# Score and weighted-sum tiles in pairs, and a table of ranks, in a four-layer graph attention kernel

## The chip, the cores and the metric

The kernel runs on one core of a Trainium2 chip. Its time is the device time of one execution in microseconds (us); lower is better. TensorE (PE) multiplies, VectorE (DVE), ScalarE (ACT) and GpSimd (POOL) do the elementwise work, and SyncE (SP) issues most of the transfers.

## The reference

`x` has 128 graphs of 64 nodes with 512 features each, `adj` says for each graph which nodes see each other. Four layers follow one another, each with a residual:

```
h = relu(layernorm(x));  x = x + layer_l(h, adj)
layers 0 and 2: q, k, v = h@Wq, h@Wk, h@Wv          (4 heads of 64)
                softmax(where(adj, q k^T / 8, -max)) v  @ Wo + bo
layer 1:        a second layernorm (gamma, beta), 8 heads of 64, out projection 512 x 512
layer 3:        m = h@map^T + b;  n = m normalized per head;  cos = n n^T > 0.1, masked
                p = softmax(where(mask, -1e10, (m@q^T)(m@k^T)^T / 8)), masked
                out = relu((cos * p) (h@gcn^T + b) @ W^T / (sum(cos * p) + 1))     (8 heads of 64)
```

All is f32.

## The kernel before

**Tiling.** The 8192 rows of `x` make 16 groups `s` of 512 rows: 8 graphs, two to a block of 128 rows, four blocks to a group. A step is a pair (layer, group). `x` goes back to memory between layers.

**One step.** `loads` fetches `x`; `layernorms` normalizes; `transposes`, `moves` and `turned_tokens` turn the tokens into `hT`. The projections are done by `winograd`: seven products of half-size blocks in place of eight, each of four matmuls (line 636), in the PSUM tiles `mA` (four of the seven, one after another in the same tile, each copied out by ACT before the next begins), `mB` and `mC` (added by DVE, line 666). `front` then takes the mask (`masks`) and makes the scores (`scores`, line 954): matmuls on quarters of the array, 64 x 64, four side by side, 32 of them to fill a `sc` tile of two PSUM banks. Layers 0 and 2 have one such unit for a group, layers 1 and 3 two. `softmax_parts` (965 to 984) masks the tile, takes the maximum and, in layers 1 and 3, subtracts it into `E`, after which the `sc` tile is free; in layers 0 and 2 ACT's exponential reads the tile sixteen times. `divide` (997) scales the rows on POOL. `turns` brings `E` into its transpose `F` (eight ACT copies, line 1006, and a DVE transpose, 1010). `attention` makes the weighted sums `po` (line 1127), again 32 quarter matmuls into a tile of the same ring as the scores, copies them out and multiplies by the output weights. In layer 3 `front` also makes the cosines, which fill a `sc` tile too and are read by `neighbours` (1234), and `last` makes `po3` (1272), which `finish` (1179) adds to the residual. `norms` (896) gives the lengths for the cosines, `add_rows` (869) adds a bias row to the layer 3 values.

**PSUM.** Eight banks: one `sc` tile of two, three `ma` tiles and three `mm` tiles of one bank each (`mm` holds `mB`, `mC` and some small tiles).

**The order.** Every part of the work is a generator that yields what it needs: an event, or an instruction with an engine and an assumed duration. `Order.run` is a planner that runs while the program is written: it takes the generator whose instruction can start first by its own clock and, among equals, the one with the smaller `prio`:

```python
s = min(self.live, key=lambda s: (s.start(self.free), s.prio))
s = self.urgent(s) or s
if eng == "pe":
    at += DRAIN * (self.quads != s.quads())
```

The order in which it takes them is the order of the instructions in each engine's queue, which the chip then keeps. A `Ring` gives tiles out in turn: the n-th tile comes free when its user sets its event. What one generator writes between two yields stays together; `scores` and `attention` yield once for every 8 matmuls and `last` for every 4 (`quads`), so that others can come between.

Of the kernel before, what the change touches and what calls it, by code (L numbers as in the profile page):

```python
# [14 lines left out]
P = 128  # L15
D = 512
N = 64
# [9 lines left out]

DRAIN = 0.1

# [45 lines left out]
class Order:  # L75
# [13 lines left out]
    def step(self, s):  # L89

        self.now = s.ready
        while True:
            try:
                r = next(s.gen)
            except StopIteration:
                self.live.remove(s)
                return
            if isinstance(r, Event):
                if r.t is None:
                    s.op = None  # L100
                    self.live.remove(s)
                    r.waiting.append(s)
                    self.held.add(s)
                    return
                s.wait_for(r.t)
                self.now = s.ready
            else:
                s.op = r
                return
# [101 lines left out]
def gnn_stack(ctx: ExitStack, tc: tile.TileContext, a: dict, out: bass.AP):  # L211
# [32 lines left out]
    ps = bass.MemoryType.PSUM  # L244
    r_sc = ring("sc", 1, [P, 2, 512], space=ps)
    r_ma = ring("ma", 3, [P, 512], space=ps)
    r_mm = ring("mm", 3, [P, 512], space=ps)

# [99 lines left out]
    def weights():  # L348
        for key, parts in units:
            if key == "q1":  # L350
                yield p_ready[0, 0]
# [104 lines left out]
    def loads(steps):  # L456
        for l, s in steps:
            if l > 0:
                yield x_done[l - 1, s]
# [22 lines left out]
    def layernorms(steps, half):  # L482

        for l, s in steps:
            yield l_ready[l, s, half]
            whole, xe = loaded.pop((l, s, half))
# [9 lines left out]
    def turned_tokens(l, s):  # L496
# [25 lines left out]
        moved = od.event()  # L522
        od.spawn(part(blocks[:3], moved), 3)
        yield from part(blocks[3:], None)
# [14 lines left out]
    def moves(steps):  # L539

        fe = None
        for l, s in steps:
            for half in range(2):
                yield n_ready[l, s, half]
# [29 lines left out]
    def transposes(steps):  # L574

        for l, s in steps:
            if (l, s) in by_dma:
                h = yield from by_vector(l, s)
            elif (l, s) in turned:
                h = yield from turned_tokens(l, s)  # L580
            else:
                h, h_done[l, s] = yield from r_h.new("hT")
                hT[l, s] = h
# [158 lines left out]

    def unit(A, BT, tokens_out, out_):

        used, begun = od.event(), od.event()
        od.spawn(winograd(A, BT, tokens_out, out_, used, begun), 5)
        yield begun
        return used

    st, p_ready, s_ready, p_used, o_used, turn = {}, {}, {}, {}, [], []  # L750

    def projections(steps):
        for l, s in steps:
# [4 lines left out]
            if l in (0, 2):  # L758
                yield w_ready[f"qk{l}"] if (l, s) != (0, 0) else first_w
                qk, z["qk_done"] = yield from r_qk.new("qk")  # L760
                used = yield from unit(W[f"qk{l}"], (*BT, w_sums[f"qk{l}"]), False, Out(quarters(qk)))
                od.spawn(when([used], s_ready[l, s], w_done[f"qk{l}"] if end else None), 0)
# [4 lines left out]
                def vv(i, k, V=V):  # L767
                    return V[:, 2 * k:2 * k + 2, i * P:(i + 1) * P]
                es = [used, (yield from unit(v_part(W[f"vo{l}"]), (*BT, wv_sums[l]), True, Out(vv)))]
                z["v"] = V  # L770
                od.spawn(when(es, p_ready[l, s], t_done[l, s], h_done[l, s]), 0)
            elif l == 1:
                es = []
                for n in "qk":
                    yield w_ready[f"{n}1"]
                    o, z[f"{n}_done"] = yield from r_qk.new(f"{n}T")
                    es.append((yield from unit(W[f"{n}1"], (*BT, w_sums[f"{n}1"]), False,
                                               Out(quarters(o)))))
                    od.spawn(when([es[-1]], w_done[f"{n}1"] if end else None), 0)
# [5 lines left out]
                def vv(i, k, V=V):  # L785
                    return V[:, 2 * k:2 * k + 2, i * H:(i + 1) * H]
                es.append((yield from unit(W["v1"], (*BT, w_sums["v1"]), True, Out(vv))))
                z["v"] = V
# [22 lines left out]
    def map_part(s, z):  # L811
        yield w_ready["map3"]
        if s == 1:
# [3 lines left out]
        z["m_ready"] = yield from unit(W["map3"], (*hB[3, s], w_sums["map3"]), False,  # L817
                                       Out(quarters(mT), map_b))
        z["m_sums"], z["n_ready"], z["m_used"] = od.event(), od.event(), od.event()
        od.spawn(when([z["m_ready"]], w_done["map3"] if s == NG - 1 else None), 0)  # L820
        od.spawn(sums_after(z["m_ready"], quarters(mT), z, z["m_sums"], s == NG - 1), 1)
        lengths.append(z["n_ready"])
        od.spawn(norms(mT, s, z["m_ready"], z["n_ready"], z["m_used"]), 3)

    lengths = []

    def of_map(n, s, z, bias):
# [4 lines left out]
        z[f"{n}_ready"] = yield from unit(W[f"{n}3"], (quarters(z["n"]), z["T"], w_sums[f"{n}3"]),  # L832
                                          False, Out(quarters(o), bias))

# [7 lines left out]
    def sem_part(s, z):  # L842
# [4 lines left out]
        def sv(i, k):  # L847
            return V[:, 2 * k:2 * k + 2, i * H:(i + 1) * H]
        used = yield from unit(W["sem3"], (*hB[3, s], w_sums["sem3"]), True, Out(sv))
        rows = od.event()  # L850
# [90 lines left out]

    def scores(lT, rT, npair, blocks):
        S, e = yield from r_sc.new("sc")
        nb = len(blocks)
        for b, t in enumerate(blocks):
            for c in range(npair):
# [3 lines left out]
                for g in range(2):  # L950
                    k = slice(t * P + g * N, t * P + (g + 1) * N)
                    for par in range(2):
                        r = slice(par * N, (par + 1) * N)
                        nc.tensor.matmul(S[g * N:(g + 1) * N, par, col],  # L954
                                         lT[r, c, k], rT[r, c, k], start=True, stop=True)
        return S, e

# [141 lines left out]
    def units_of(l):  # L1099
# [3 lines left out]
        return nch, [list(range(u, u + per)) for u in range(0, TB, per)]  # L1103

    def attention(l, s):
        z = st.pop((l, s))
# [3 lines left out]
        got = {("e", k): od.event() for k in range(2)}  # L1110
        od.spawn(residuals(l, s, w_ready[wkey], got), 2)
        O, oe = yield from r_m.new("oT")
        O = O.rearrange("p c t -> p (c t)")
        for u, blocks in enumerate(units):
            yield z["pt_ready", u]
            pt, pte = z["pt", u]
            po, poe = yield from r_sc.new("po")
            for b, t in enumerate(blocks):
# [13 lines left out]
            if u == len(units) - 1:  # L1132
                z["v_done"].set()

            yield act(1.02)
            nc.scalar.copy(O[:, u * 1024:(u + 1) * 1024].rearrange("p (i g q) -> p g i q", g=2, q=N),
                           po.rearrange("p g (i q) -> p g i q", q=N))
            poe.set()
        O = O[:, 0:1024 * len(units)].rearrange("p (k c n) -> p k c n", k=2, n=H)

# [9 lines left out]
        if o_used:  # L1150
            yield o_used.pop()
        used = yield from unit(wo, (ov, T, w_sums[wkey]), True, Residual(got))
        o_used.append(used)
# [34 lines left out]
    def front(l, s):  # L1188
# [8 lines left out]
        masked = [od.event() for _ in units]  # L1197
        od.spawn(when(masked, me), 0)
        for u, blocks in enumerate(units):
            E, e = yield from r_e.new("E")  # L1200
            S, se = yield from scores(z["q"], z["k"], 2 * nch, blocks)
            if u == len(units) - 1:
# [3 lines left out]
            m = mask[:, blocks[0]:blocks[0] + len(blocks)]  # L1206
            z["e", u], z["exp", u] = (E, e), od.event()
            od.spawn(softmax(l, z, u, S, se, m, masked[u]), 1)
        if l < 3:
            return  # L1210
        yield z["n_ready"]
        found = [od.event() for _ in units]
        od.spawn(when(found, nfe), 0)
        for u, blocks in enumerate(units):
            C, ce = yield from scores(z["n"], z["n"], 4, blocks)
            if u == len(units) - 1:
                z["m_done"].set()
            nfv = nf[:, blocks[0]:blocks[0] + 2, :].rearrange("p b k -> p (b k)")
            od.spawn(neighbours(z, u, C, ce, nfv, found[u]), 1)

# [32 lines left out]
    def last(s):  # L1253
        z = st[3, s]
        got = {("e", u): od.event() for u in range(2)}
        od.spawn(last_residuals(s, got), 2)
        for u in range(2):
            yield z["pt_ready", u]
            pt, pte = z["pt", u]
            yield p_ready[3, s]  # L1260

            po, poe = yield from r_sc.new("po3")
            for b in range(2):
# [17 lines left out]
    def fronts(steps):  # L1281
        for l, s in steps:
            yield from front(l, s)

    def turns(steps):

        for l, s in steps:
            yield p_used[l, s]
            z = st[l, s]
            for u in range(len(units_of(l)[1])):  # L1290
                yield z["e_ready", u]
                z["pt", u] = yield from transposed(*z["e", u])
                z["pt_ready", u].set()

    def attentions(steps):
        for l, s in steps:
            yield p_used[l, s]
            if l < 3:
# [5 lines left out]
    for k in steps:  # L1304
        for e in (p_ready, s_ready, p_used, h_ready, f_ready, x_done):
            e[k] = od.event()
        for half in range(2):
            l_ready[(*k, half)], n_ready[(*k, half)] = od.event(), od.event()
    with tc.manual_schedule():
        od.spawn(weights(), 4)  # L1310
        od.spawn(loads(steps), 4)
        for half in range(2):
            od.spawn(layernorms(steps, half), 4)
        od.spawn(moves(by_dma), 3)
        od.spawn(transposes(steps), 3)
        od.spawn(projections([k for k in steps if k[0] < 3]), 5)
        od.spawn(fronts(steps), 1)
        od.spawn(turns(steps), 1)
        od.spawn(attentions(steps), 2)
        od.run()  # L1320
# [45 lines left out]
```

## Time and profile before

| | |
|---|---|
| median of 3 runs | 2753.67 us (2753.2 to 2754.24) |
| profiled execution | 2752.83 us, span of its instructions 2750.6 us |
| PE busy | 2682.1 us, 98% of the span |
| DVE, ACT, POOL busy | 1950.9, 1885.3, 1608.4 us |
| granted clock, mean over the span | 0.991 |

A busy time is the sum of the stretches in which an engine worked. Idle time of an engine counts only where it makes the one wait that sets the end. A line such as `L636` is a line of the kernel's source; `mA<-hT,w_q` are the tile written and those read; `x8` is how many instructions the row holds. Every f32 matmul of the source is two instructions in the trace. `issue` is time in which nothing was waited for that the trace shows.

### The profile page before, as it was taken

To read this page: it belongs to the slowest core of one execution; us is meant where nothing else is said; L and a number is where in the kernel's file an instruction comes from. 1 tells how busy PE (TensorE), PEld (TensorE's weight loads), DVE (VectorE), ACT (ScalarE), POOL (GpSimd) and SP (SyncE) were. 2 spreads that over 40 slices of the span, in tenths; PEclk is the share of its full clock that TensorE was granted. 3 is DMA by queue.
4 is the path that set the end of the run, shared out by engine and by line. 5 is a ranking of instruction groups with operands and counts; after the bars stand their busy time and mean duration, and the time that the engine had idled before them with its cause. 6 is when DMAs were issued, how large, how long until landed. Compare 5 with 4: busy or idle time off the path is not lost.

```text
span 2750.6 us, 63739 instructions
## 1 busy us (share of the span) xinstructions
PE 2682.1 (98%) x26280; PEld 2323.4 (84%) x26280; DVE 1950.9 (71%) x2836; ACT 1885.3 (69%) x3517; POOL 1608.4 (58%) x1242
## 2 busy tenths in 40 slices
PE   7999999999999999999999999999999999999997
PEld 6888888888888888888898888888888888888876
DVE  6888888676666667665678888747776777667655
ACT  5667677678777777776667676656677666776644
POOL 4776767554445445545666767676565555655533
PEclk9999999999999999999999999999999999999998
DMA  5566663221112112212456665323223322233121
GB/s 164 143 178 142 161 170 106 78 77 65 48 63 78 48 48 71 71 48 96 135 126 167 149 163 150 121 100 88 65 64 87 97 69 64 64 87 87 49 64 47
DMA packets 396978, 267.90 MB, mean 97 GB/s; under 512 B 260496, under 2 KB 305552, under 8 KB 396688
## 3 DMA queue, kind: packets, MB, share of 16 engines
q1 hardware_dynamic: 382176, 249.37, 33.1%
q10 hardware_dynamic: 14512, 14.47, 1.7%
q8 instruction: 206, 3.38, 0.5%
q14 instruction: 84, 0.69, 0.1%
HBM read 166.77 MB, written 67.63 MB: 85 GB/s over the span
## 4 chain that ended last, share of the span: by engine, by line
PE 84%; DVE 7%; ACT 3%; POOL 3%; DMA 2%; issue 1%; SPq 0%; ACTq 0%; DVEq 0%; POOLq 0%
PE mA L636 43%; PE mC L636 21%; PE mB L636 11%; PE sc L954 4%; PE po L1127 2%; PE po L1272 1%; ACT F L1006 1%; ACT E L977 1%; DVE sc L965 1%; DVE mx L971 1%; PE mmn L896 1%; POOL t L346 1%; DVE st L423 1%; POOL E L997 0%; PE ptr L593 0%
## 5 line engine op out<-in xcount | busy, mean ns | idle before, releaser
L1006 ACT COPY F<-E 32x512 f32<-32x512 f32 x768 | 472.5, 615 | 47.5 <-POOL E L997 36.0
L1075 POOL TENSOR_TENSOR xres<-xres,u 128x512 f32<-128x512 f32 x192 | 258.9, 1356 | 246.2 <-ACT u L1070 237.9
L1054 POOL TENSOR_TENSOR xres<-xres,u 128x512 f32<-128x512 f32 x192 | 252.6, 1339 | 40.0 <-DMA xres<-x 27.5
L439 ACT ACTIVATE xin<-xin,rs 128x512 f32<-128x512 f32 x320 | 248.4, 812 | 22.5 <-DVE rs L432 20.3
L519 ACT COPY hT<-xin 32x512 f32<-32x512 f32 x364 | 224.1, 616 | 6.4
L423 DVE BATCH_NORM_STATS2 st<-xin 128x6 f32<-128x512 f32 x320 | 214.1, 669 | 9.5 <-DMA xin<-x 5.2
L430 POOL TENSOR_TENSOR rs<-rs,mhalf 128x2 f32<-128x2 f32 x160 | 115.9, 728 | 132.7 <-DVE rs L428 120.5
L653 ACT COPY v<-mA 128x256 f32<-128x256 f32 (+1 forms) x192 | 94.5, 492 | 137.4 <-PE mA L636 133.7
L346 POOL TENSOR_TENSOR t<-hT,t 128x512 f32<-128x512 f32 x126 | 183.3, 1454 | 8.9
L346 POOL TENSOR_TENSOR t<-hT 128x512 f32<-128x512 f32 x63 | 80.7, 1281 | 168.8 <-DVE hT L529 96.2
L997 POOL TENSOR_TENSOR E<-E,sm 128x1024 f32<-128x1024 f32 x64 | 125.6, 1963 | 85.5 <-ACT xin L439 43.1
L1070 ACT COPY u<-mA 128x512 f32<-128x512 f32 x144 | 84.6, 587 | 116.5 <-PE mA L636 112.0
L1010 DVE STREAM_TRANSPOSE F<-F 128x1024 f32<-128x1024 f32 x96 | 118.4, 1234 | 60.6 <-ACT F L1006 60.6
L991 DVE TENSOR_REDUCE sm<-E 128x16 f32<-128x1024 f32 x128 | 154.9, 1210 | 6.9 <-ACT E L984 5.7
L977 ACT ACTIVATE E<-sc,mx 128x64 f32<-128x64 f32 x512 | 124.9, 362 | 32.7 <-DVE mx L974 32.7
L516 POOL COPY hT<-xin 32x512 f32<-32x512 f32 x84 | 64.4, 766 | 138.1 <-ACT xin L439 135.8
L636 PE MATMUL mA<-w_vo,t 128*128 128x128 f32 (+1 forms) x768 | 135.4, 312 | 8.1 <-ACT v L653 4.2
L636 PE MATMUL mA<-hT,w_qk 128*128 128x256 f32 x512 | 129.3, 392 | 7.5 <-DVE hT L569 6.0
L997 POOL TENSOR_TENSOR E<-E,f 128x1024 f32<-128x1024 f32 x32 | 61.1, 1910 | 111.7 <-DVE f L995 95.0
L636 PE MATMUL mA<-t,w_qk 128*128 128x256 f32 x512 | 122.7, 380 | 1.4 <-DVE t L343 1.4
L869 POOL TENSOR_TENSOR v<-v,gcn_row 128x512 f32<-128x512 f32 x64 | 81.2, 1300 | 71.9 <-ACT v L653 71.9
L636 PEld LDWEIGHTS mA<-w_vo,t 128*128 128x128 f32 x768 | 108.7, 191 | 16.9 <-ACT v L653 5.1
(223 smaller groups left out, 7493.7 us busy)
## 6 DMA issues: line engine op xcount, KB each, us to landing
x<-xres SPq DMA_DIRECT2D x96, 512.0 KB
xin<-x SPq DMA_DIRECT2D x96, 512.0 KB
xres<-x SPq DMA_DIRECT2D x64, 512.0 KB
F<-xin SPq DMA_DIRECT2D x448, 64.0 KB
xres<-in_x SPq DMA_DIRECT2D x32, 512.0 KB
u<-rs SPq DMA_DIRECT2D x128, 128.0 KB
xres<-x SPq DMA_DIRECT2D x64, 256.0 KB
out<-xres SPq DMA_DIRECT2D x64, 256.0 KB
```

Source lines behind the costliest of these rows:

```text
L346: nc.gpsimd.tensor_tensor(o, i0, i1, ALU.subtract)
L423: nc.vector.bn_stats(st, v[:, t, :])
L439: nc.scalar.activation(v[:, t, :], v[:, t, :], func, bias=rs[:, 2, t:t + 1], scale=rs[:, 0, t:t + 1])
L519: nc.scalar.copy(o, v)
L636: nc.tensor.matmul(o, l, r, start=(first and m == 0 and k == 0), stop=(k == KC - 1), skip_group_check=True)
L977: nc.scalar.activation(E[:, i, :], S3[:, i, :], AF.Exp, bias=mx[:, i:i + 1], scale=0.125)
L991: nc.vector.tensor_reduce(o, E, AX.X, ALU.add)
L997: nc.gpsimd.tensor_mul(E, E, sm[:, :, None].to_broadcast([P, 16, N]))
L1006: nc.scalar.copy(F[g * N + 32 * k:g * N + 32 * (k + 1), :, 32 * i:32 * (i + 1)], E[g * N + 32 * i:g * N + 32 * (i + 1), :, 32 * k:32 * (k ...
L1010: nc.vector.transpose(F, F)
L1054: nc.gpsimd.tensor_add(xr[:, t, :], xr[:, t, :], bo[l])
L1075: nc.gpsimd.tensor_add(v, v, both(u))
```

## The change

The PSUM is cut anew: two `sc` tiles (four banks), two `ma` and two `mm`. `front` takes the tiles of both units of a group before it makes the scores of either, so that the planner can put the 64 matmuls in a row; the cosines likewise, and `last` and `attention` the weighted sums. In `attention` the copy out of a `po` tile becomes a generator of its own, `out_of`, so that the second sum need not wait for it. In layers 0 and 2 `front` waits, as the planner sees it, for the transposes of the group before (`pt_done`), so that its scores and that group's weighted sums come at one time. The planner's fixed `prio` numbers give way to a table by kind of work and layer (`RANK`), and its assumed cost of a change between the two kinds of matmul goes from 0.1 to 0.15. No instruction is added or taken away.

```diff
-DRAIN = 0.1
+DRAIN = 0.15
+RANK = {
+    "load": (5.5, 5.5, 3, 5.5),
+    "norm0": (4, 4, 5.5, 4),
+    "norm1": (4, 4, 4, 3.5),
+    "move": (5, 2, 1, 5.5),
+    "turn": (3.5, 3, 1, 3.5),
+    "part": (5, 5, 5, 5),
+    "weight": (0.5, 6, 3.5, 1),
+    "proj": (5, 5, 5, 5),
+    "out": (0.5, 5, 5, 2),
+    "front": (0.5, 0.5, 0.5, 1.5),
+    "soft": (1.5, 4, 1, 1.5),
+    "near": (0.5, 3, 3, 0.5),
+    "trans": (3.5, 2, 5.5, 2),
+    "att": (5, 2, 2, 5),
+    "res": (2.5, 1.5, 5, 6),
+    "msum": (3, 0.5, 1.5, 0.5),
+    "length": (4, 5.5, 2, 1.5),
+}
+def rank(what, l):
+    return Rank(RANK[what][l])
...
+            if isinstance(r, Rank):
+                s.prio = r
+            elif isinstance(r, Event):
...
-    r_sc = ring("sc", 1, [P, 2, 512], space=ps)
-    r_ma = ring("ma", 3, [P, 512], space=ps)
-    r_mm = ring("mm", 3, [P, 512], space=ps)
+    r_sc = ring("sc", 2, [P, 2, 512], space=ps)
+    r_ma = ring("ma", 2, [P, 512], space=ps)
+    r_mm = ring("mm", 2, [P, 512], space=ps)
...
     def loads(steps):
         for l, s in steps:
+            yield rank("load", l)
...
-    def scores(lT, rT, npair, blocks):
-        S, e = yield from r_sc.new("sc")
+    def scores(S, lT, rT, npair, blocks):
...
+    def out_of(O, u, po, poe, copied):
+        yield act(1.02)
+        nc.scalar.copy(O[:, u * 1024:(u + 1) * 1024].rearrange("p (i g q) -> p g i q", g=2, q=N),
+                       po.rearrange("p g (i q) -> p g i q", q=N))
+        poe.set()
+        copied.set()
     def attention(l, s):
...
+        room, copied = [], []
+        for u in range(len(units)):
+            yield z["pt_ready", u]
+        for u in range(len(units)):
+            room.append((yield from r_sc.new("po")))
         for u, blocks in enumerate(units):
-            yield z["pt_ready", u]
             pt, pte = z["pt", u]
-            po, poe = yield from r_sc.new("po")
+            po, poe = room[u]
...
+            copied.append(od.event())
+            od.spawn(out_of(O, u, po, poe, copied[-1]), 0)
+        for e in copied:
+            yield e
...
     def front(l, s):
...
+        room = []
+        if l in (0, 2) and s > 0:
+            yield pt_done[l, s - 1]
+        for u in range(len(units)):
+            z["e", u] = yield from r_e.new("E")
+        for u in range(len(units)):
+            room.append((yield from r_sc.new("sc")))
         for u, blocks in enumerate(units):
-            E, e = yield from r_e.new("E")
-            S, se = yield from scores(z["q"], z["k"], 2 * nch, blocks)
+            S, se = room[u]
+            yield from scores(S, z["q"], z["k"], 2 * nch, blocks)
...
+        room = []
+        for u in range(len(units)):
+            room.append((yield from r_sc.new("cos")))
         for u, blocks in enumerate(units):
-            C, ce = yield from scores(z["n"], z["n"], 4, blocks)
+            C, ce = room[u]
+            yield from scores(C, z["n"], z["n"], 4, blocks)
...
     def last(s):
...
         for u in range(2):
             yield z["pt_ready", u]
+        yield p_ready[3, s]
+        room = []
+        for u in range(2):
+            room.append((yield from r_sc.new("po3")))
...
     def turns(steps):
...
+            pt_done[l, s].set()
...
-        od.spawn(projections([k for k in steps if k[0] < 3]), 5)
-        od.spawn(fronts(steps), 1)
+        od.spawn(projections([k for k in steps if k[0] < 3]))
+        od.spawn(fronts(steps))
```

The streams that took a fixed number when they were started now yield their rank at each step, as `loads` does above.

## The prediction

> **What bounds the kernel now.** I read the page first, then the windows of the stretches that fall behind, then the TensorE timeline of a quiet stretch, and last the chain of waits and the tail.
>
> ```profile
> PE 2682.1 (98%) x26280; PEld 2323.4 (84%) x26280; DVE 1950.9 (71%) x2836; ACT 1885.3 (69%) x3517; POOL 1608.4 (58%) x1242
> PE 84%; DVE 7%; ACT 3%; POOL 3%; DMA 2%; issue 1%; SPq 0%; ACTq 0%; DVEq 0%; POOLq 0%
> ```
>
> TensorE (PE) is busy 98% of the span and is 84% of the chain that ended last; no other engine passes 71%. So time comes off only where PE needs less of it or stands still less. Where it stands still, by stretch:
>
> ```profile
> 60.00:80.00 20.00, 12.91 (x109) 10.29 (x108) 11.99 (x20) 12.87 (x33) 12.84 (x11) 0.83 0.66 152
> ...
> 2600.00:2620.00 20.00, 17.13 (x246) 13.08 (x245) 14.15 (x17) 7.19 (x13) 9.94 (x8) 0.83 0.01 3
> 2660.00:2680.00 20.00, 15.05 (x270) 12.68 (x263) 13.42 (x11) 4.52 (x8) 7.68 (x6) 0.83 0.35 89
> 2720.00:2751.00 31.00, 11.48 (x282) 9.36 (x280) 13.57 (x19) 11.60 (x19) 8.70 (x6) 0.70 0.40 103
> ```
>
> The first number after the stretch's length is PE's busy time; the third from the end is the granted clock. From 600 to 1300 us PE idles 0.5 us in all, so the steady part holds almost no waits. Instead, it pays for changing between whole-array products (128*128) and products on quarters of the array (64*64, `sc` and `po`):
>
> ```profile
> 1001.94 1.89 PE L636 MATMUL mA<-hT,w_q 128*128 128x256 f32 x8
> 1003.76 1.16 PE L1127 MATMUL po<-F,v 64*64 64x64 f32 x64
> 1004.86 1.99 PE L636 MATMUL mB<-hT,w_q 128*128 128x256 f32 x8
> 1006.69 1.89 PE L636 MATMUL mA<-t,w_q 128*128 128x256 f32 x8
> 1008.41 1.89 PE L636 MATMUL mC<-t,w_q 128*128 128x256 f32 x8
> ```
>
> Read the starts. Eight whole-array matmuls follow each other 1.72 us apart (1006.69 to 1008.41). The quarter run starts 1.82 us after its predecessor (0.09 late), the next whole-array group starts 1.10 us after the quarter run, and the one after that 1.83 us later (0.10 late). By the single starts in the trace the 64 quarter matmuls lie 943 ns from first to last, 15.0 ns each, so they need 0.96 us by themselves and 0.14 of the 1.10 is the way back. Going there and back costs 0.09 + 0.14 + 0.10 = **0.33 us per run**; 148 of the 169 runs of 64 that stand cleanly between whole-array products show this within a nanosecond.
>
> Two stops late in the kernel are the score tile itself, which has one buffer:
>
> ```profile
> 2607.88 0.69 DVE m L666
> 2608.58 1.14 DVE mx L971
> 2609.72 0.02 issue
> 2609.74 1.24 DVE E L981
> 2610.97 0.14 issue
> 2611.11 1.20 PE sc L954 x64
> 2612.31 0.02 issue
> 2612.33 1.24 DVE Cf L1234
> 2613.57 0.04 issue
> 2613.61 1.99 PE sc L954 x64
> ```
>
> PE ended its products at 2607.86 and waits for VectorE (DVE) to take the maximum and subtract it (L981), since only then may the next tile overwrite `sc`; then again for L1234. The second run of 64 takes 1.99 instead of 0.96 us: the clock was halved. The same happens at 2660.66 (L965, L971, L981 in a row). Against the pitches above, PE loses 13.0 us between 2600 and 2680, 10.5 between 60 and 80.
>
> **The change, part by part.** The order of instructions on each engine in the changed program can be read without running it. It holds the same instructions, number for number (13,204 matmuls in the source, each f32 one being two in the trace); only their order, the PSUM tiles and the waits differ.
>
> Switches: the order shows 221 quarter runs before and 158 after. By quarters of PE's work: 50 to 57, 51 to 28, 55 to 41, 65 to 32. So "all in one" is true of layer 3 and mostly of layer 1; in much of layer 0 both `sc` and `po` are cut into 8 and 24 matmuls with whole-array products between, which is worse than before. 63 runs x 0.33 = 20.8 us of PE time, and PE has no slack to hide it in.
>
> Up to the end of the last cosine run: two of those runs lie behind it, so 61 x 0.33 = 20.1 less; but 3.0 us of `sem3` products that stood behind it now stand ahead. Net **-17.1**.
>
> From there to the end only one chain counts. Before: cosines end at 2717.0, span ends at 2750.6, 33.6 us. After, from the queues' order and the rows' durations: DVE Cf 1.23, product 1.22, row sum 1.21, two additions to v 1.38, f and reciprocal 0.45, second Cf 1.23, row sum 1.21, four `xres` 2.6 (now ahead of the second product), product 1.22, row sum 1.21, f and reciprocal 0.45: 13.4. Then POOL E 1.9, eight ACT copies 5.0, DVE transpose 1.25, `po3` 2.0, `xres` 1.3, and 5.0 for the stores as now: 16.5. With hand-overs 30.1 us. POOL's row additions for the last v (4.93 us, which delayed E before, 2728.99 to 2733.92) end before E is ready. **-3.5**.
>
> The stops at 2606-2671: two `sc` tiles let the next score start while DVE still works on the last. In the new order the last scores and the cosines of the same group lie 8 to 12 us of PE work apart, and DVE needs about 7.4 for the two subtractions ahead. One place stays tight: scores right behind `po3` (about 1 us short, twice). I take 2 of the 13.0 as remaining: **-11**. Bounds: -13 and 0.
>
> Start and layer 0: PE waited 6 us for `hT` (L569), behind the DMA copies of `xin` to `F`. On SP's queue those copies now come ahead of the second half of the next `xin` and of `xres`; but the ~5 us of `w_k` DMA are still there. And between 100 and 600 PE loses 12.8 us, often 0.4 to 1.8 at the first `vo` products waiting for ACT's copies; by the new order those distances are longer. I take **-5** of 23; bounds -12 and +6 (the same stop a second time).
>
> New stops: at -0, nothing; at most one of the kind above for each of the three layer changes. I take **+4**, the price of the smallest of today's (4.4 us at 1360-1380); bounds 0 and 13.
>
> What is costed at nothing. PSUM: `ma` and `mm` go from three to two tiles. Cover: by the order a new `mC` waits for a DVE addition that lies 6.9 us of PE work back (4.4 for the narrow `vo`), against an ACT copy of 0.6, an addition of 0.69 and at most two DVE instructions of 1.2 ahead; the wait for ACT's copy within a unit (1.7) is the same as before. Uncovered, each of the 224 product units would pay. The Trainium skill speaks against this part: "Perfetto Trace Analysis", section "Matmuls", wants independent groups to rotate through PSUM banks so that evacuation overlaps. All eight banks are still used, four now by scores. By that rule alone, priced with the nearest row (ACT's copy of 0.59, uncovered once per unit), it would cost 224 x 0.6 = 134 us and end near 2850; by the distances it costs none. I take the distances.
>
> `pt_done` puts the scores of s behind the transposes of s-1. It only orders the issue, no semaphore wait is added on `sc`. Scores to `po` of one group shrinks from 37 to 29 us of PE work; DVE, ACT and POOL work between is about 17.5 us by the rows. The waiting scores hold up only the softmax of s. That leaves 11 us of cover; each us short of it would cost 32, one per group of layers 0 and 2. The split evacuation (`out_of`) gives `po` back a run later; its reader, the output product, needs both parts anyway. On POOL every wait of PE lies over 10 us back; nothing there becomes tight.
>
> The clock: in both late stops the granted clock is 0.83 over 20 us, so (1 - 0.83) x 20 = 3.4 us are lost each time. "TensorE: Matmul & The Clock Gate", section "What's actually happening", has full rate return after one busy window of about 3.4 us, a loss of 1.7. With its figure the late stops would be worth 3.4 us less and the result 2724; I keep the trace's.
>
> Sum: -17.1 - 3.5 - 11 - 5 + 4 = -32.6. The profiled execution took 2752.83 us (span 2750.6), 0.84 below the median of the runs; 2752.83 - 32.6 = 2720.2, against the median 2721.
>
> **The rivals.**
> Only the switches and the tail pay: -20.6, and one more stop of 6.8. The waits only move, for a planner that closes one gap opens another. For it: DVE is at 71%, and the scores now come in pairs, 5 us of DVE work each. Against: the gaps between sc and its readers are longer. 2732 to 2740.
>
> Everything goes well: -17.1 - 3.5 - 13 - 12, no new stop: 2708.
>
> Slower: PSUM starvation. PE at the first `mB` or `mC` of a unit, behind DVE's addition, pays from 0.15 us per unit on (32.6 / 224) more than is won; at 0.25 us it is +56 - 32.6 = +23, 2777. For it: waits of PE on DVE rise from 395 to 586. Against: 0.5 us idle in 700 today, and distances of 4.4 to 6.9.
>
> The change doesn't do what it says: in layer 0 it does not, as counted. That is in the sum.
>
> **How the numbers follow.** Likeliest case (2712 to 2730) 0.5; only switches (2730 to 2741) 0.24; all goes well (2704 to 2712) 0.14; stops eat nearly all (2741 to 2759) 0.07; starvation 0.05. Two runs apart by 0.2%, 5.5 us, are what a measurement here can tell from no change. Faster 0.92, same 0.03, slower 0.05. The range 2706 to 2740 leaves out about 0.2.
>
> **What would show it.** In the profile after: PE busy lower by about 20 us; quarter runs of x128 in layers 1 and 3, 2.05 us from their start to the next whole-array product (1.10 for x64 now); granted clock 1.00 from 2570 to 2660; the last `po3` starting some 22 us after the cosines (25 now). PE waits "mC <- DVE" or "mB <- DVE" of many tenths in every unit would prove it wrong; so would granted clock below 0.9 in more than four stretches.

## The result, and the profile after

The changed kernel takes **2716.52 us** (median of 4 runs, 2716.26 to 2716.95) against 2753.95 for the kernel before in the same session: ratio 0.9863, 95% interval 0.9846 to 0.9880. Run a second time in another session it took 2715.74 against 2750.46, ratio 0.9869 (0.9852 to 0.9886). The profiled execution took 2716.46 us, its span is 2714.7 us, 35.9 less than before.

From the page, the busy times and the shares of the chain that ended last:

```profile
PE 2651.8 (98%) x26280; PEld 2316.3 (85%) x26280; DVE 1908.4 (70%) x2836; ACT 1887.6 (70%) x3517; POOL 1612.0 (59%) x1242
PE 92%; DVE 3%; DMA 2%; ACT 1%; POOL 1%; issue 1%; SPq 0%; ACTq 0%; POOLq 0%; DVEq 0%
```

The same 26280 matmuls keep PE busy 30.3 us less, and PE is now 92% of the chain instead of 84%: less of the time is somebody else's. The windows where PE stood still before, and a new one (PE, weight loads, DVE, ACT, POOL, granted clock, DMA share, GB/s):

```profile
60.00:80.00 20.00, 19.81 (x231) 17.79 (x229) 17.22 (x29) 12.35 (x33) 16.98 (x14) 1.00 0.46 126
1290.00:1320.00 30.00, 22.09 (x129) 18.70 (x119) 13.47 (x15) 7.15 (x12) 17.61 (x17) 0.83 0.41 122
2600.00:2620.00 20.00, 20.00 (x97) 16.63 (x96) 9.46 (x14) 16.02 (x31) 10.36 (x3) 1.00 0.19 55
2660.00:2680.00 20.00, 20.00 (x212) 17.53 (x211) 10.31 (x12) 11.14 (x19) 7.71 (x7) 1.00 0.00 1
```

The two late stops are gone (20.00 of 20.00 busy, clock 1.00); the stretch at 60 to 80 has 19.81 us of PE instead of 12.91. A new stop has come at 1290 to 1320: 7.9 us idle. In a quiet stretch TensorE's timeline shows a pair:

```profile
2570.52 2.10 PE L1336 MATMUL po<-v,F 64*64 64x64 f32 x128
2572.54 1.99 PE L673 MATMUL mA<-hT,w_map 128*128 128x256 f32 x8
```

A run of 128 starts at 2570.52 and the next whole-array product at 2572.54: 2.02 us for what took 2 x 1.10 as two runs.

The time can be booked in three terms. PE's losses are what it falls behind the pitches of the prediction (0.216 us per whole-array matmul, 0.015 per quarter, 0.33 per quarter run), summed from its first matmul to its last by the single starts in the trace:

| | before | after | difference |
|---|---|---|---|
| quarter runs, 0.33 us each | 221 | 158 | -20.8 us |
| PE's losses | 69.8 us | 50.5 us | -19.3 |
| first matmul | 11.2 us | 15.2 us | +4.1 |
| span | 2750.6 us | 2714.7 us | -35.9 |

That the terms add up to the span proves nothing: the losses are by their making what the other terms leave. What stands on its own is the number of runs, which can be counted, and the price of one, which section 3 measures.

The losses by stretch: 0 to 600 us went from 30.6 to 21.4, 1300 to 1900 from 11.9 to 21.1, 1900 to 2000 from 5.1 to -0.6 (a little faster than the pitches), 2600 to 2680 from 13.0 to 2.6; each other hundred moved by about 1 us or less.

### The profile page after: what moved, and what is told of

Same layout as the page of the kernel before. It is cut to its first block, busy times and chain, and to the rows that moved or that the text cites. A ratio compares the mean times of both kernels' runs of the same rounds, so it can differ in the third digit from the quotient of the medians.

```text
span 2714.7 us, 63736 instructions
## 1 busy us (share of the span) xinstructions
PE 2651.8 (98%) x26280; PEld 2316.3 (85%) x26280; DVE 1908.4 (70%) x2836; ACT 1887.6 (70%) x3517; POOL 1612.0 (59%) x1242
## 4 chain that ended last, share of the span: by engine, by line
PE 92%; DVE 3%; DMA 2%; ACT 1%; POOL 1%; issue 1%; SPq 0%; ACTq 0%; POOLq 0%; DVEq 0%
PE mA L673 47%; PE mC L673 24%; PE mB L673 12%; PE sc L994 4%; PE po L1177 2%; PE cos L994 1%; PE po L1336 1%; PE mmn L937 1%; DMA xres<-x 1%; PE ptr L630 0%; ACT F L1045 0%; ACT E L1016 0%; DVE sc L1004 0%; POOL xres L1093 0%; DVE mx L1010 0%
## 5 line engine op out<-in xcount | busy, mean ns | idle before, releaser
L1045 ACT COPY F<-E 32x512 f32<-32x512 f32 x768 | 473.4, 616 | 35.7 <-POOL E L1036 24.9
L463 POOL TENSOR_TENSOR rs<-rs,mhalf 128x2 f32<-128x2 f32 x160 | 134.7, 844 | 209.4 <-DVE rs L461 197.2
L378 POOL TENSOR_TENSOR t<-hT 128x512 f32<-128x512 f32 x63 | 82.0, 1301 | 128.8 <-DVE hT L564 46.5
L673 PEld LDWEIGHTS mA<-w_vo,t 128*128 128x128 f32 x768 | 110.5, 191 | 11.4 <-ACT v L690 1.9
L1010 DVE TENSOR_REDUCE mx<-sc 128x16 f32<-128x1024 f32 x96 | 116.9, 1218 | 2.2
```

The lines of the kernel that those rows point to most:

```text
L378: nc.gpsimd.tensor_tensor(o, i0, i1, ALU.subtract)
L463: nc.gpsimd.tensor_tensor(rs[:, 0, :], rs[:, 1, :], mhalf[:, :2], ALU.pow)
L673: nc.tensor.matmul(o, l, r, start=(first and m == 0 and k == 0), stop=(k == KC - 1), skip_group_check=True)
L1045: nc.scalar.copy(F[g * N + 32 * k:g * N + 32 * (k + 1), :, 32 * i:32 * (i + 1)], E[g * N + 32 * i:g * N + 32 * (i + 1), :, 32 * k:32 * (k ...
```

## The experiments

The theory: TensorE pays for each change to quarter products and back; the pairs save those changes, and two score tiles let the late stops go, as long as the planner keeps the waits around the merged runs covered. The rivals: the PSUM cut starves the product units; the second score tile alone, or the table of ranks alone, makes the gain; a change by itself costs nothing, and all the time comes from waits. Five parts of the answer follow.

### 1. Do two `ma` and two `mm` tiles starve PE?

The kernel before, with only this edit; one score tile stays, and two banks are left empty.

```diff
-    r_ma = ring("ma", 3, [P, 512], space=ps)
-    r_mm = ring("mm", 3, [P, 512], space=ps)
+    r_ma = ring("ma", 2, [P, 512], space=ps)
+    r_mm = ring("mm", 2, [P, 512], space=ps)
```

> The kernel before with two mA and two mm tiles in place of three, all else kept (221 quarter runs, as before). Theory (the smaller rings cost nothing): TensorE's waits stay, 2754 within 6 us. Rival (starvation of PSUM): from 0.15 us per product unit on, 224 units, at least +34 us, 2788 or more, with waits of PE at mB and mC on DVE.

Measured: 2754.96 us against 2752.43, ratio 1.0012 (1.0004 to 1.0020). What PE waits for in it (total, times, longest):

```profile
PE po L1272 <- DVE F L1010: 9.7, 1, 9.7
PE mA L636 <- ACT v L653: 7.7, 10, 1.9
```

The large waits are those of the kernel before (10.0 and 7.0 us there). `mC` waits for DVE only twice, 0.8 us in all, and `mB` never, where 224 units that each paid 0.15 us would have given 34 us. The cost is 0.1%, so the starvation is refuted for the kernel before; in the changed kernel no wait of `mB` or `mC` for DVE shows at all.

### 2. One part of the change alone

`b_psum`: the kernel before with the new PSUM cut (two score tiles, two `ma`, two `mm`), tiles still taken one by one, old numbers in the planner.

```diff
-    r_sc = ring("sc", 1, [P, 2, 512], space=ps)
-    r_ma = ring("ma", 3, [P, 512], space=ps)
-    r_mm = ring("mm", 3, [P, 512], space=ps)
+    r_sc = ring("sc", 2, [P, 2, 512], space=ps)
+    r_ma = ring("ma", 2, [P, 512], space=ps)
+    r_mm = ring("mm", 2, [P, 512], space=ps)
```

> The kernel before with the new cut of the PSUM alone (two score tiles, two mA, two mm), the tiles still taken one by one, the old fixed numbers. Its order has 185 quarter runs, so 36 fewer: -11.9 us. Theory (a run costs 0.33 us, stops late in the kernel come from the single score tile): -11.9 and -10 for the stops between 2600 and 2680, but its order puts more of TensorE's waits on ACT close behind the copy that they wait for (sum of the shortfalls 221 us against 72 before, most of it in layers 0 to 1), which costs some of that: 2740 within 12. Rival (the ranks make the gain): 2750 or more.

Measured: 2765.72 us, ratio 1.0066 (1.0041 to 1.0091). The theory's 2740 is missed by 26 us. The rival's number, 2750 or more, holds, but its reason, that the ranks make the gain, does not survive the next run.

`b_rank`: the table of ranks and the assumed 0.15 us in the kernel before, with its one score tile, the tiles taken one by one, and no `pt_done`. The numbers given to the planner change, in this way everywhere:

```diff
-DRAIN = 0.1
+DRAIN = 0.15
+RANK = {...}
...
-        od.spawn(winograd(A, BT, tokens_out, out_, used, begun), 5)
+        od.spawn(winograd(A, BT, tokens_out, out_, used, begun), prio)
```

> The changed kernel's table of ranks and 0.15 on the old cut of the PSUM (one score tile, three mA, three mm), tiles taken one by one, no wait for the transposes of the group before. Its order has 224 quarter runs, three more than before. Theory (the gain is switches and the second score tile): +1.0 for switches, the stops late in the kernel stay, 2752 within 12. Rival (the ranks make the gain): 2725 or less.

Measured: 2798.76 us, ratio 1.0181 (1.0159 to 1.0203): the table alone makes this kernel slower. Both accounts (2752, and 2725 or less) missed it.

`a_flat`: the changed kernel, its pairs and its PSUM cut, with the old fixed numbers written into every column of the table; `pt_done` and the assumed 0.15 us stay.

```diff
-    "load": (5.5, 5.5, 3, 5.5),
-    "norm0": (4, 4, 5.5, 4),
+    "load": (4, 4, 4, 4),
+    "norm0": (4, 4, 4, 4),
...
-    "front": (0.5, 0.5, 0.5, 1.5),
+    "front": (1, 1, 1, 1),
...
-    "att": (5, 2, 2, 5),
+    "att": (2, 2, 2, 2),
```

> The changed kernel with the old fixed numbers in its table, the same in all layers (0.15 kept). Its order has 116 quarter runs, 42 fewer than the changed kernel. Theory (0.33 us per run): switches 105 x 0.33 = 34.7 us below before, but the waits on ACT are nearer than in the changed kernel (132 short ones against 24, shortfalls of 222 us against 27, in layers 0 and 1 above all), so the ranks pay by waits: slower than the changed kernel, 2717 to 2745. Rival (switches are all): 2703, 13.9 us faster than the changed kernel.

Measured: 2743.32 us, ratio 0.9968 (0.9958 to 0.9978), inside the theory's range.

The same booking for all of them, each against the kernel before (the sums come out by their making, as above):

| kernel | quarter runs | runs x 0.33 | losses | first matmul | sum | span measured |
|---|---|---|---|---|---|---|
| `b_psum` | 185 | -11.9 | 94.6 (+24.9) | -0.2 | +12.8 | +13.1 |
| `b_rank` | 224 | +1.0 | 111.6 (+41.8) | +4.2 | +47.0 | +47.0 |
| `a_flat` | 116 | -34.7 | 91.7 (+21.9) | +0.3 | -12.5 | -12.4 |
| changed kernel | 158 | -20.8 | 50.5 (-19.3) | +4.1 | -36.0 | -35.9 |

`a_flat` is the telling row: it has 42 runs fewer than the changed kernel, worth 13.9 us, and its span is 23.5 us longer (its median 26.8). The number of runs is not what decides. What PE waits for most; `b_psum`, then `b_rank`, then `a_flat`:

```profile
PE po L1127 <- DVE F L1010: 22.2, 11, 3.6
```

```profile
PE po L1174 <- ACT E L1016: 20.1, 6, 6.9
```

```profile
PE po L1177 <- DVE F L1049: 20.6, 9, 2.6
```

In all three the weighted sum stands at the head of TensorE's queue too early, but not for the same reason. In `b_psum` and `a_flat` it waits for `F`, the last step of its own softmax. In the kernel before that wait (L1127 for L1010) came once, 0.2 us. Most of it lies in layer 1, and the order there shows why. From the last score matmul of a unit to the first matmul of its weighted sum, both by their starts, median over the 16 groups:

| layer 1 | first unit | second unit | PE idle before a sum of layer 1 |
|---|---|---|---|
| kernel before | 26.3 us | 27.5 us | none |
| `b_psum` | 22.0 | 27.5 and 31.4 in turn | 2.3 to 3.5 us, at seven places from 584 to 1246 |
| `a_flat` | 25.0 and 31.1 in turn | 27.5 and 31.1 in turn | 2.2 to 2.5 us, at seven places from 573 to 1227 |
| changed kernel | 65.2 | 65.3 | 1.4 us, once |

The stops lie at the second unit of every second group, the 27.5 of these rows, and that figure holds the stop: without it only some 25 us of work lie between (27.5 less 2.8 and less 2.2). The kernel before put 27.5 us of work there and did not wait, but it had little to spare: from the end of `F` to the start of the sum it had 0.9 us at the second units (median), the sums that stop have 0.1, and the changed kernel has 16.7.

So with the old numbers the planner, offered a second score tile, puts some sums nearer behind their scores; with the table it lets some 40 us more of other work come between. This is what the table buys, and the second score tile is what makes the distance affordable. In the kernel with one tile (`b_rank`) the sums of layer 0 stand 63 us behind their scores, and their softmax is done 38.7 us ahead of them (medians). They wait all the same, for the tile:

```profile
228.07 0.46 PE L994 MATMUL sc<-qk 64*64 64x64 f32 x16
233.06 3.38 ACT L1016 ACTIVATE E<-sc,mx 128x64 f32<-128x64 f32 x16 [5.10 <-DVE mx L1013]
236.49 1.98 PE L1174 MATMUL po<-F,v 64*64 64x64 f32 x64 [6.89 <-ACT E L1016]
```

The scores of a later group were written into the one tile just ahead of the sum, and the sum gets it only when ACT's sixteen exponentials have read them: 6.9 us idle here, and again at 418. Late scores and cosines wait for the tile too (up to 3.7 us, from 2658 to 2717). In `b_psum` the late stops did go (losses of 3.5 us between 2600 and 2700, where the kernel before has 13.0 between 2600 and 2680), as the second tile was to bring; the early layers cost more. Behind the first matmul, the largest waits of the changed kernel are others:

```profile
PE po L1336 <- DVE F L1049: 12.4, 2, 7.2
PE mC L673 <- ACT u L1109: 7.9, 1, 7.9
```

The first lies in the tail; the second is the new stop. So the parts work together only: cut alone +0.7%, table alone +1.8%, cut and pairs (with `pt_done`) -0.3%, all of it -1.4%.

### 3. What one change of kind costs

The changed kernel, with one whole-array product put between the two score runs (and the two cosine runs) of a pair: 48 places. The product writes into a tile whose 32 quarter products are about to overwrite it.

```diff
+            if u == 1:
+                for _ in range(1):
+                    nc.tensor.matmul(S[:, 0, 0:P], ident, ident, start=True, stop=True)
             S, se = room[u]
```

`d_2` has `range(2)`. The second product changes nothing of the kind, so the difference between the two kernels is the product itself, and what the first adds beyond it is one way there and back.

> The changed kernel with one small whole-array product (128 x 128, two matmuls of 112 ns in the trace) between the two units of a group wherever scores or cosines come in pairs: 48 places in layers 1 and 3, written into the second unit's tile before its scores, which overwrite it. No other instruction moves. It breaks up to 48 paired runs again. Theory (a run costs 0.33 us, by the changed kernel's runs of 128 0.35): 48 x (0.22 + 0.35) = 27 us slower than the changed kernel, about 2744. Rival (the switches are covered and the gain is in the waits): 48 x 0.22 = 11 us or less, 2727.

> As the run with one small product in each of the 48 places, with two of them in a row. It separates the product's own cost from the way there and back. Theory: 10.8 us more than with one, so 2755, and what one costs less this difference, 16 to 17 us, is the price of 48 runs. Rival (the products themselves cost 0.57 each and the switch nothing): 27 us more than with one, 2771.

Measured: `d_1` 2743.46 us, ratio 0.9973 (0.9962 to 0.9984); `d_2` 2754.82 us, ratio 1.0012 (1.0005 to 1.0019). PE's losses stay as they were (50.7 and 51.6 against 50.5), so the added time is all TensorE's own. TensorE's timeline of `d_1`, then of `d_2`:

```profile
2082.72 1.16 PE L994 MATMUL sc<-kT,qT 64*64 64x64 f32 x64
2083.81 0.49 PE L1260 MATMUL sc<-ident 128*128 128x128 f32 x2
2084.22 1.16 PE L994 MATMUL sc<-kT,qT 64*64 64x64 f32 x64
2085.32 1.56 PE L673 MATMUL mB<-hT,w_map 128*128 128x256 f32 x6
```

```profile
2090.22 1.16 PE L994 MATMUL sc<-kT,qT 64*64 64x64 f32 x64
2091.31 0.71 PE L1260 MATMUL sc<-ident 128*128 128x128 f32 x4
2091.95 1.16 PE L994 MATMUL sc<-kT,qT 64*64 64x64 f32 x64
2093.05 1.56 PE L673 MATMUL mB<-hT,w_map 128*128 128x256 f32 x6
```

By the starts in these rows a pair takes 2.60 us with one product and 2.83 with two, and the run of 128 shown above took 2.02. More finely, from the last matmul before the pair to the end of the first eight whole-array matmuls after it, less the pitches of these, a pair takes 2.222 us without a product between (70 of 72 clean pairs of the changed kernel), 2.798 with one (38 of 45) and 3.022 with two. The second product is 0.224, so a way there and back is 2.798 - 2.222 - 0.224 = **0.352 us**. A second way to it, within the changed kernel: a run of 128 takes 2.222, a run of 64 takes 1.288; the 64 further matmuls cost 0.934, and the remaining 1.288 - 0.934 = 0.354 are the change. The prediction's 0.33 was 0.02 short: it measured the pitch of a quarter product from the first to the last start of a run of 64, 15.0 ns, where further ones cost 14.6. 63 runs are 22.3 us instead of 20.8.

### 4. `pt_done`

The changed kernel without the wait of the scores for the transposes of the group before.

```diff
-        if l in (0, 2) and s > 0:
-            yield pt_done[l, s - 1]
```

> The changed kernel without the planner's wait of the scores in layers 0 and 2 for the transposes of the group before. Its order has 133 quarter runs, 25 fewer. Theory (runs and waits trade; by the queues' order the shortfalls of TensorE's waits on ACT grow from 27 to 117 us): 8.9 us less for switches, 15 to 25 more for waits, 2719 to 2735. Rival (the switches decide): 2708.

Measured: 2720.94 us, ratio 0.9888 (0.9872 to 0.9905). Without it the planner makes 133 runs in place of 158, which is worth 25 x 0.35 = 8.8 us, and PE's losses rise from 50.5 to 62.8, most of it in this wait, which the changed kernel has not:

```profile
PE sc L994 <- ACT qk L690: 8.0, 12, 1.0
```

Scores now come as soon as their `q` and `k` are copied, and wait for the copy 12 times. The two profiled spans lie 4 us apart, in opposite terms: the line that was to bring the runs together leaves more runs and fewer waits. The two were not run side by side, and the intervals of their ratios overlap, so that `pt_done` gains time on the whole is not shown; that 25 runs fewer bring no gain is.

### 5. The new stop at 1297, and the late start

The chain of waits of the changed kernel at the stop, in order of time:

```profile
1295.55 4.42 DMA xres<-x
...
1300.10 0.42 POOL xres L1093
...
1301.31 1.27 POOL xres L1114
...
1302.61 0.69 DVE xres L703
1303.30 1.14 DVE E L1020
...
1305.43 0.58 ACT u L1109
```

Read from the end: the product waits for ACT's copy `u`; ACT had an exponential ahead of that copy, which needs DVE's `E` (L1020); DVE had `xres` (L703) ahead of `E` in its queue, which waited for POOL, and POOL for the transfer that brings the residual `x` of the last group of layer 1. That transfer starts at 1295.55. SP's queue tells why:

```profile
1277.98 17.53 SPq L590 DMA_DIRECT2D F<-xin  x12
1295.55 1.02 SPq L1089 DMA_DIRECT2D xres<-x  x1
```

It stood behind twelve small copies that took 17.53 us to issue. `r_res` gives the residual of layer 1 a better rank, so that the planner puts its load earlier; the order on PE and the 158 runs are the same.

```diff
-    "res": (2.5, 1.5, 5, 6),
+    "res": (2.5, 0.5, 5, 6),
```

> The changed kernel with one number of the table changed: residual loads of layer 1 at 0.5 in place of 1.5. TensorE's order is the same, 158 runs; on SP's queue the load of the last group's residual at the end of layer 1 now stands ahead of seven of the copies of xin to F. Theory (the stop of 8 us at 1297.8 is that load, held up behind those copies and then by the weights of layer 2): the stop and its halved clock, 10.8 us, go, 2706. Rival (the weights' transfer holds everything up in any order, or the wait is DVE's or ACT's own): 2716 as now.

Measured: 2709.72 us (2705.66 to 2712.22), ratio 0.9847 (0.9831 to 0.9862). Run again beside the changed kernel on the same chip:

> The changed kernel once more, beside the next one on the same chip, so that the two can be compared without the kernel before between them. Theory: 2716 within 4 us, with the stop of 8 us at the end of layer 1 at the same place.

> The changed kernel with the residual loads of layer 1 at 0.5 once more, beside the changed kernel on the same chip. Theory (the stop at the end of layer 1 is a load kept waiting on SP's queue): 7 to 11 us faster than the changed kernel beside it. Rival (the 7 us of the run before were another chip): within 3 us of it.

Measured: changed kernel 2715.74 us (2713.00 to 2717.66), `r_res_2` **2707.22 us** (2702.74 to 2708.51), ratio to before 0.9838 (0.9823 to 0.9854). The two ranges don't overlap; this is the fastest version of the study, 8.5 us below the changed kernel. SP's queue and the window of the stop in `r_res_2`:

```profile
1277.14 4.25 SPq L590 DMA_DIRECT2D F<-xin  x5
1281.44 0.62 SPq L1089 DMA_DIRECT2D xres<-x  x1
```

```profile
1290.00:1320.00 30.00, 29.34 (x166) 25.49 (x159) 16.44 (x19) 16.03 (x26) 18.91 (x17) 1.00 0.57 181
```

The load is issued 14 us earlier, PE idles 0.7 us in place of 7.9, and the clock isn't lowered.

The start: the first matmul comes at 15.2 us instead of 11.2.

```profile
PE ptr L630 <- ACT xin L472: 15.2, 1, 15.2
```

In the chain of the changed kernel DVE's first work is the sums of the `w_qk` weights (L364), which wait for their transfer, and the first layernorm stands behind them:

```profile
2.92 7.01 DMA w_qk<-in_Wk
...
9.95 0.70 DVE w_qk L364
```

Two edits on top of `r_res`: `g_weight` gives the weights of layer 0 a worse rank, `g_norm` gives its layernorms a better one.

```diff
-    "weight": (0.5, 6, 3.5, 1),
+    "weight": (4, 6, 3.5, 1),
```

```diff
-    "norm0": (4, 4, 5.5, 4),
+    "norm0": (0.4, 4, 5.5, 4),
```

> The changed kernel with residual loads of layer 1 at 0.5 (as in the run before that moved them) and the weights of layer 0 at 4 in place of 0.5, so that the four additions to w_qk on DVE no longer stand ahead of the first group's normalization. 164 quarter runs. Theory (those additions make TensorE's first matmul 4.1 us later than in the kernel before, 15.2 against 11.2): first matmul at 11.2, but six runs more (+2.1) and a nearer wait for hT and the copies at 44 to 62 us: 2703 to 2712. Rival (the loads of x alone set the start): first matmul at 15 as now and 2712 or more.

> The changed kernel with residual loads of layer 1 at 0.5 and the first normalization of layer 0 at 0.4 in place of 4. 138 quarter runs, 20 fewer than the changed kernel. Theory (runs and waits trade): -7.0 for the runs, -3 for the start, but the shortfalls of the waits on ACT grow from 27 to 74 us, among them one of 6.6 us at 30 us: 2703 to 2713, no better than the run with the residual loads alone. Rival (the switches decide): 2700.

Measured: `g_weight` 2709.38 us, ratio 0.9843 (0.9821 to 0.9865), the same as `r_res`; `g_norm` 2712.66 us, 0.9855 (0.9828 to 0.9881). In `g_weight` the first matmul is back at 11.4 us, and the losses of the first 120 us rise from 12.4 in `r_res` to 16.5, as much as the start had gained. A wait that `r_res` doesn't have tells where it went:

```profile
PE ptr L630 <- ACT xin L472: 11.4, 1, 11.4
PE mA L673 <- DVE hT L605: 4.4, 1, 4.4
```

The late start costs nothing between these two: PE waits at the start, or a little later for the `hT` of the third group. `g_norm` starts at 12.5 us and loses 25.8 us in its first 120: putting the layernorms first only moved the wait and made it longer. Its time can't be told from that of `r_res`, for it also has 20 runs fewer.

## Why the prediction was right

Forecast 2721, measured 2716.5, inside the likeliest case (2712 to 2730). Point by point, in us of the span:

| step | forecast | measured |
|---|---|---|
| runs up to the last cosines | -17.1 | 61 x 0.354 = 21.6 less, 3.0 of `sem3` more: -18.6 |
| from there to the end | -3.5 | 33.6 to 30.2: -3.3 |
| stops at 2600 to 2680 | -11 | 13.0 to 2.6: -10.4 |
| start and layer 0 | -5 | -9.2, and +4.1 by the later first matmul: -5.1 |
| new stops | +4 | +9.2 (1300 to 1900) |
| stop at 1940 | not named | -5.7 |
| sum | -32.6 | -33.9; the span -35.9 |

The switch price held up as a mechanism: section 3 measures it alone, in 48 added places. It was mis-sized by 0.02 us per run, for the reason given there.

The stops at 2600 to 2680 and the tail came out as worked, the tail by the same chain; three steps of it, the first `Cf`, the four `xres` in one go ahead of the second product, and `po3`:

```profile
2689.14 1.16 DVE Cf L1295
...
2691.34 2.48 DVE xres L1229 x4
...
2706.30 2.02 PE po L1336 x64
```

`po3` starts 21.8 us after the cosines' end (2684.46), forecast 22, 25 before.

The late stops were priced by the trace's clock loss (3.4 us each) and not by the single busy window that the prediction took from the Trainium skill ("TensorE: Matmul & The Clock Gate", section "What's actually happening"). In the trace before, the granted clock is halved for 6.8 us at each of the two stops, not for 3.4, and the 10.4 us won lie nearer to the trace's -11 than to the -7.6 that one window for each stop would have made, by estimate.

The start came out at its number, though by a split that the text did not have: 9.2 less in the waits after the first matmul, 4.1 more ahead of it. The later start was not foreseen at all, so that the net came out is luck; `g_weight` shows only that the start and the waits behind it make up for each other.

New stops were under-sized: 9.2 for 4. The step "the price of the smallest of today's" failed; what came was one stop of the larger kind, at a layer change as the text said, but released by a transfer on SP's queue. The sum had asked what SP's new order does at the start only. The stop at 1940, left out of the sum, paid that back: two misses of opposite sign, so the total is closer than its parts, by luck.

What was costed at nothing held. The two tiles of `ma` and `mm` cost 0.1% on the kernel before (section 1). The rule of the Trainium skill that the prediction weighed there ("Perfetto Trace Analysis", section "Matmuls"), which priced at one uncovered copy per unit would have ended near 2850 by the prediction's estimate, does not decide here: two tiles still rotate, and no product unit of the changed kernel waited for DVE's additions.

The cover behind `pt_done` held too, but with less to spare than the text counted. In layers 0 and 2 the scores lie 29.6 and 30.3 us ahead of their sums (median; 37.5 before), as the text had it (29), and PE does not wait there. But the text set 17.5 us of DVE, ACT and POOL work against that, which left 11 us; by the trace `F` is done 5.4 and 4.6 us ahead of the sum (12.2 before), so these steps take some 25 us with the waits between them. In `a_flat`, at 26.6 us, only 2.2 are left. The text also did not ask which edit made these distances, and did not price the cover of layer 1 at all, 0.9 us in the kernel before: that is where the change could have failed.

Of the signs listed: PE busy fell by 30, not 20 (the runs are 22 of it; the rest was not taken apart); the run of 128 takes 2.02 to the next product (2.05 forecast); the clock is 1.00 in both late windows; no `mC` or `mB` waits for DVE. Two 20-us windows lie below a clock of 0.9, the one at 1300 and the last.

One figure needs a note: the 13,204 matmuls of the source make 26280 in the trace because the 128 transposes among them are one instruction each.

What stays open: why the stop at 1940 went was not tried by itself (the first sum of layer 3 waited 3.3 us for DVE there, and 0.3 in the changed kernel), and the 2.0 us between the sum and the span are spread over the trace in tenths.

## What to carry to other kernels

Count how often TensorE changes between whole-array and quarter products in its queue and price a change by two runs of different length in the trace. Then ask of every merge whether the softmax, copy or load that used to lie between is still covered, from the end of that work to the start of what needs it: a kernel with 42 changes fewer was about 27 us slower here where it was not. When a planner writes the order, its priorities and the tiles it may use are one edit: alone each made the kernel slower. And read the reordering on the queue that issues the transfers too: a load behind twelve small copies stopped TensorE for 7.9 us, and one number in a table took the stop away.

## What the runs showed that was not expected

- Taking a wait away saved 25 runs and won nothing: without `pt_done` 12 us more of losses eat them up.
- A second score tile, with two banks taken from rings that hardly needed them, made the kernel before 0.7% slower: the planner used it to put every second group's second sum of layer 1 closer behind its scores (some 25 us of work for 27.5).
- Winning back the 4 us of the later first matmul gained nothing: a wait came 50 us later.
- The lowered clock moves with the stops: before it lies at 67, 1367, 1944, 2613 and 2664 us, after at 100, 550, 1301 and 1397, for 3.4 to 10.2 us each, besides the tail.
